# A four-layer graph network on one core: where the third chunk of layer 2 gets its first loads, and where pieces of layer 3 stand between its pairs

## The chip, the cores and the metric

The kernel runs on one core of one Trainium2 chip. TensorE (PE) multiplies matrices into PSUM, VectorE (DVE), ScalarE (ACT) and GpSimd (POOL) do the elementwise work, SyncE (SP) issues nearly all transfers from HBM. The metric is the device time of one execution in microseconds; the time of a kernel is the median of its runs.

## The reference

Four layers follow each other on 3327 nodes with 64 features; each adds its result to its input and normalises every row. All four use the same 3327 x 3327 matrix `adj`.

```python
# layer 0
neigh = jnp.matmul(adj, features) / (adj.sum(axis=1, keepdims=True) + 1.0)
x = _layernorm(x + jnp.concatenate([x, neigh], axis=-1) @ W.T)
# layer 1: w = adj / deg; agg = einsum('ij,ijc->ic', w, logmap(x_i, x_j)); then weight, bias, expmap
x = _layernorm(x + _L1_gnn_ref(x, adj, weight, bias))
# layer 2
deg = jnp.clip(jnp.sum(adj, axis=1, keepdims=True) + 1.0, 1.0, None)
h_neigh = (adj @ X + X) / deg
out = jax.nn.relu(jnp.concatenate([X, h_neigh], axis=1) @ W + b)
x = _layernorm(x + out / jnp.maximum(jnp.linalg.norm(out, axis=1, keepdims=True), 1e-12))
# layer 3
support = input @ weight
mask = (adj != 0)
rank = jnp.cumsum(mask, axis=1); deg = rank[:, -1:]; k = jnp.minimum(deg, 100.0)
pos = rank - (deg - k)
w = mask * jnp.where(pos > 0, 0.5 ** (k - pos), 0.0)
x = _layernorm(x + w @ support + bias)
```

## The kernel before

**Tiles and chunks.** The nodes are padded to 26 blocks of 128. `adj`, transposed by the host, is cut along its rows' nodes into four chunks of 832 columns. One load (`load_adj`, L289) brings a pair of blocks of one chunk, 128 x 2 x 832 numbers, 832 KB, into one of four buffers with the tag `adj`; a load into a list of two tiles (L285) is two transfers of one block each. All of these are on SP's queue, in the order in which the program makes them, and a load waits there until its buffer has been read.

**Layer 2** goes through the chunks in the order `ORDER2 = (2, 3, 1, 0)`: `n == 0` is chunk 2, `n == 1` chunk 3, `n == 2` chunk 1, `n == 3` chunk 0. In this document the first, second, third and fourth chunk are meant in that order. A chunk is 13 pairs; the place of a pair in its chunk's order is called its position, `i`. `aggregate_pair` (L455) multiplies one pair into an accumulator, with four matmuls, each of which stands in the trace as two rows. At the end of a chunk `keep_sums` copies the accumulator to SBUF (L439), and `epilogue2` multiplies the weights (L1226) and makes the features of that chunk's blocks, among them `parts`, a sum of three bfloat16 terms for layer 3.

**Ranks and masks.** Layer 3's weights come from ranks, which for the second chunk are counted while its pairs go by: DVE makes a mask of each pair (L481) in one of ten buffers with the tag `m16`, PE counts it (L527) two pairs later, DVE carries the count on (L513) and ACT writes the ranks (L537). The ranks' last row is mended by `last_rows`, with small DMAs on POOL's queue and three DVE steps (L554 to L556).

**Layer 3** is cut into 52 pieces, each a pair of blocks of one chunk. `expand` turns a piece's ranks into `bits` (L1288 on ACT, L1290 on DVE, also in `m16` buffers; the letters of `L3_ENGINES` and `L3_FIRST` name the engine), and `piece` multiplies them with `parts` in twelve matmuls (L1313). A piece needs the features of its two blocks alone, so pieces run beside layer 2: `L3_AMONG` says behind which positions of the third and fourth chunk one stands. The first piece makes nine pieces' bits before itself (`BITS_AHEAD`, `L3_FIRST`), which DVE and ACT begin behind the last mask and the last ranks; every piece then makes those of the ninth piece after it. Pieces 0 to 5 need blocks of the first chunk only, piece 6 is the first that needs a block of the second. The other pieces follow layer 2, and `epilogue3` ends each chunk: weights (L1330), sum with the features (L1337), squares (L403) into the one buffer `sq`, their sum (L404), a root (L417) with three short DVE steps (L418 to L420), the output (L1347) and its transfer (L1351). The last chunk is ended in two halves of three and four blocks.

The order of the work on an engine is the program's, rearranged when it is built by a planner with costs of its own; `issue_after` fixes the order of two instructions of one engine. At run time each engine keeps its order.

The edit touches `sum_of_squares` and `table_root` (which other epilogues also call, without the new arguments), and, inside `layers_2_and_3`, `epilogue2`, `expand`, `piece`, `epilogue3` and the loop over `ORDER2`.

Of the kernel before, what the change touches and what calls it, by code (L numbers as in the profile page):

```python
# [20 lines left out]
FP = mybir.dt.float32  # L21
# [4 lines left out]
AF = mybir.ActivationFunctionType  # L26
# [5 lines left out]
P = 128  # L32
NB = 26
NP = NB * P
D = 64
CH = 832
HC = CH // 2
NCH = NP // CH
# [6 lines left out]
GB = 7  # L45
# [53 lines left out]
L3_ENGINES = "VSVVS"  # L99
BITS_AHEAD = 9  # L100

L3_FIRST = "VVVVSVVSV"

L3_AMONG = {2: range(6, 13), 3: range(13)}


L3_LEFT = 16
# [5 lines left out]
def four_gnn_layers_kernel(  # L113
# [279 lines left out]
                issue_after(ins, behind)  # L393
        return True

    def sum_of_squares(y, nb, s, alone=False):

        width = y.shape[2]
        sq = small.tile([P, GB, D], FP, name="sq", tag="sq", bufs=1)
        if alone:  # L400
            nc.vector.tensor_mul(sq[:, 0:nb, 0:width], y, y)
        else:
            nc.scalar.activation(sq[:, 0:nb, 0:width], y, AF.Square)  # L403
        return nc.vector.tensor_reduce(s, sq[:, 0:nb, 0:width], axis=AX.X, op=ALU.add)  # L404

    def variance(s, work):
# [4 lines left out]

        return rsqrt(variance(s, work)[0], work)

    def table_root(s, work):

        y, h = work("root"), work("part")
        nc.scalar.activation(y, s, AF.Abs_reciprocal_sqrt, bias=ln_eps, scale=1.0 / D)  # L417
        nc.vector.scalar_tensor_tensor(h, s, D * LN_EPS, y, op0=ALU.add, op1=ALU.mult)  # L418
        nc.vector.tensor_mul(h, h, y)
        nc.vector.scalar_tensor_tensor(y, h, -3.0 * D, y, op0=ALU.add, op1=ALU.mult)  # L420
        return y
# [769 lines left out]
    def layers_2_and_3(banks, acc, done, rows, there):  # L1191


        with tc.tile_pool(name="l2m", bufs=10) as mp, tc.tile_pool(name="late", bufs=1) as late:
# [24 lines left out]
            def epilogue2(c, x2, behind=None):  # L1219


                b0, b1_, nb = blocks_of(c, GROUPS2)
                work, alone = Work(nb), c == ORDER2[-1]
                pb = per_block(banks.pair(2), nb, 2 * D)
                for k in range(nb):
                    issued = nc.tensor.matmul(  # L1226
                        pb[:, k, :], lhsT=sums[:, bass.ts(b0 + k, P)], rhs=wl2, start=True, stop=True
                    )
                    if behind is not None:
                        issue_after(issued, behind)  # L1230
# [12 lines left out]
                nc.vector.tensor_scalar_max(ss, ss, 1e-24)  # L1243
                r, k = (rsqrt(ss, work), 1.0) if alone else (table_norm(ss, work), 0.375)
                nc.vector.scalar_tensor_tensor(y, y, k, col(r, nb), op0=ALU.mult, op1=ALU.mult)
                aside.tensor_add(y, y, x2)
                ss = work("ss")
                sum_of_squares(y, nb, ss, alone)
                r, k = (deviation(ss, work), 1.0) if alone else (table_root(ss, work), -0.5 / D)
                left = node_tile("left")  # L1250
                copy = nc.vector.tensor_copy if alone else nc.scalar.copy

                for k0, k1 in ((0, 3), (3, nb)) if alone else ((0, nb),):
                    xs = x3[:, b0 + k0 : b0 + k1, :]
# [12 lines left out]
                aside.tensor_tensor(  # L1267
                    xs, xs, bias["b3"].to_broadcast([P, nb, D]), op=ALU.add
                )
                return issued  # L1270

            acc3, begun, bits_of, ranks_of = {}, set(), {}, {}

            def expand(k, behind=None):


                if k >= len(pieces):
                    return
                c, jp = pieces[k]
                bits = mp.tile([P, 2, CH], U16, name="bits", tag="m16")  # L1280
                src = last_rank if c == LATE_RANKS else rank[:, c]
                src = src[:, 2 * jp : 2 * jp + 2, :]
                bits_of[k] = bits
                engine = L3_FIRST[k] if k < len(L3_FIRST) else L3_ENGINES[k % len(L3_ENGINES)]
                if k in beside:
                    engine = "S"
                if engine == "S":
                    issued = nc.scalar.mul(bits, src, 128.0)  # L1288
                else:
                    issued = nc.vector.tensor_scalar(bits, src, 128.0, None, op0=ALU.mult)  # L1290
                if behind is not None:
                    issue_after(issued, behind[engine])
                    behind[engine] = issued

            def piece(k, behind=None):
                if not acc3:

                    for which in range(2):
                        two = banks.pair(which)
                        for half in range(2):  # L1300
                            acc3[ORDER2[which + 2 * half]] = two[:, half, :]
                    last = {"V": ranks_of[LATE_RANKS].carried, "S": ranks_of[LATE_RANKS].made}
                    for ahead in range(BITS_AHEAD):
                        expand(ahead, last)
                    step(late_rows, last["V"])
                    all_of(late_rows)
                expand(k + BITS_AHEAD)
                c, jp = pieces[k]
                bits, last = bits_of.pop(k), jp == LAST_PAIR
                for b in range(2):  # L1310
# [11 lines left out]
                begun.add(c)  # L1322
                return issued

            def epilogue3(b0, b1_, bank, behind):

                nb = b1_ - b0
                pt = per_block(bank, nb, D)
# [11 lines left out]
                )  # L1340
                work = Work(nb)
                ss = work("ss")
                sum_of_squares(y, nb, ss)
                r = table_root(ss, work)
                o = adjp.tile([P, 2, CH], FP, name="o", tag="adj").rearrange("p t c -> p (t c)")
                o = o[:, 0 : nb * D].rearrange("p (b f) -> p b f", f=D)
                nc.vector.scalar_tensor_tensor(  # L1347
                    o, y, -0.5 / D, col(r, nb), op0=ALU.mult, op1=ALU.mult
                )
# [19 lines left out]
            ahead = [half_of(wt, k) for k in range(2)] + [  # L1369
                [mp.tile([P, CH], FP, name="a1", tag="m16") for _ in range(2)] for _ in range(2)  # L1370
            ]
            ahead = [load_adj(ORDER2[1], NB // 2 - 1 - k, t) for k, t in enumerate(ahead)]
            k, made = 0, None
            for n, c in enumerate(ORDER2):
                if n > 0:
# [8 lines left out]
                for i, jp in enumerate(order):  # L1384
                    if n == 0 and i < EARLY:
                        continue
                    if n == 0 and jp in there:
                        a2 = there.pop(jp)
                    elif n == 1 and ahead:
                        a2 = ahead.pop(0)  # L1390
                    else:
                        a2 = load_adj(c, jp)
                    issued = aggregate_pair(acc, xr, a2, jp, i == 0, i == NB // 2 - 1, counted)
# [1 line left out]
                        made = epilogue2(ORDER2[0], x2, issued)  # L1395
                    if ranks:
                        mask = ranks.mask(jp, a2)
                        counted = count(masked, places, min(LATE_LAG, jp), issued)
                    if i == OWN2_AT:
                        x2, based = prologue2(c, issued)  # L1400
# [19 lines left out]
            for n in range(NCH + 1):  # L1420
                for i in range(4):
                    if n < NCH:
                        issued = piece(k)
                        k += 1
                    if n > 0 and i == (1 if n < NCH else 0):
                        b0, b1_, nb = blocks_of(ORDER2[n - 1], GROUPS2)
                        halves3 = ((b0, b0 + 3), (b0 + 3, b1_)) if n == NCH else ((b0, b1_),)
                        for half, blocks in enumerate(halves3):
                            epilogue3(
                                *blocks, banks.one((n + half) % 2), issued if n < NCH else None  # L1430
                            )
                if n < NCH:
                    keep_sums(ORDER2[n], acc3[ORDER2[n]], 0, True)

# [57 lines left out]
```

## Time and profile before

| | |
|---|---|
| median of three runs | 525.27 us (524.14 to 527.98) |
| profiled execution: time, span | 527.45 us, 525.7 us |
| busy in the span: PE, DVE, ACT, POOL | 92%, 74%, 63%, 34% |
| granted clock of PE, mean | 0.987 |
| moved by DMA | 132.52 MB, mean 252 GB/s |
| loads `adj` on SP | 137 of 832 KB, median 5.4 us from issue to landing |

The span runs from the first to the last instruction of the program; the time of the same execution is 1.75 us longer. Times inside the profile are us from the start of the span. A "busy" PE is one with a matmul in flight, and the modelled ends of matmuls overlap the starts of the next. A wait in the trace is put down to what came last.

In the span, layer 2's third chunk lies at about 403 to 440 us, the fourth at 442 to 477, the rest of layer 3 after it; the last output is issued at 522.1 us.

### The profile page before, as it was taken

How to read it: one execution, taken by the hardware profiler on the slowest of the kernel's cores; microseconds unless marked ns; L12 is line 12 of the kernel's file. 1: busy time of each engine (PE TensorE's matmuls, PEld its weight loads, DVE VectorE, ACT ScalarE, POOL GpSimd, SP SyncE). 2: the span in 40 equal slices, each digit the busy share in tenths (PEclk: the TensorE clock that was granted, in tenths of full speed). 3: DMA queues.
4: the chain of work that ended last, by engine and by line, in shares of the span. 5: the costliest groups of instructions: out<-in, count | busy, mean ns of one | idle time of the engine just before them, and what ended most of it. 6: DMA issues, size and time to landing. Idle time of an engine off the chain costs nothing.

```text
span 525.7 us, 8489 instructions
## 1 busy us (share of the span) xinstructions
PE 483.0 (92%) x3256; PEld 237.9 (45%) x3256; DVE 387.5 (74%) x705; ACT 333.7 (63%) x393; POOL 180.9 (34%) x150
## 2 busy tenths in 40 slices
PE   5999999998967999999999899899999889999993
PEld 3554344453432333433343344354564445556672
DVE  3565439879668978789789978978788956727744
ACT  1435545775868999878978896721387714337941
POOL 2001101112027788857877695600331112200000
PEclk9999999999988999999999999999999999999997
DMA  8999999998439677767866777499687898950002
GB/s 273 316 350 340 392 391 392 306 304 280 181 126 328 210 255 275 238 204 229 284 216 204 248 252 253 151 351 399 231 271 255 269 393 300 349 190 1 1 17 56
DMA packets 46179, 132.52 MB, mean 252 GB/s; under 512 B 6934, under 2 KB 7038, under 8 KB 46066
## 3 DMA queue, kind: packets, MB, share of 16 engines
q1 hardware_dynamic: 45602, 131.35, 72.2%
q0 software_dynamic: 384, 0.52, 0.3%
q8 instruction: 27, 0.44, 0.3%
q14 instruction: 22, 0.18, 0.1%
q10 hardware_dynamic: 144, 0.03, 0.0%
HBM read 130.86 MB, written 0.85 MB: 251 GB/s over the span
## 4 chain that ended last, share of the span: by engine, by line
PE 42%; DVE 16%; ACT 6%; issue 2%; DMA 1%; POOL 0%; ACTq 0%; DVEq 0%
PE two L1313 10%; PE one L455 9%; DVE p L834 7%; PE one L854 6%; PE two L823 6%; PE two L455 4%; DVE s L842 3%; ACT s L847 3%; ACT s L848 2%; PE two L527 2%; DMA adj<-in_adjt_dram 1%; PE two L1226 1%; PE one L1330 1%; PE two L891 1%; DVE mask L513 1%
## 5 line engine op out<-in xcount | busy, mean ns | idle before, releaser
L849 POOL TENSOR_TENSOR s<-s,p 128x832 f32<-128x832 f32 x67 | 130.1, 1957 | 45.4 <-ACT s L848 34.9
L834 DVE SCALAR_TENSOR_TENSOR p<-two,adj 128x832 f32<-128x832 f32 x100 | 101.0, 1018 | 18.3 <-issue 13.6
L823 PE MATMUL two<-uw 64*128 64x416 f32 x416 | 91.1, 552 | 13.6 <-DVE s L842 7.2
L537 ACT ACTIVATE rank<-two,last_bias 128x832 uint8<-128x832 f32 x78 | 71.7, 952 | 45.4 <-PE two L527 23.1
L455 PE MATMUL one<-adj,x0w 128*64 128x416 f32 x416 | 82.8, 524 | 2.8 <-DMA adj<-in_adjt_dram 1.4
L854 PE MATMUL one<-s,xu 128*64 128x416 f32 x416 | 85.2, 525 | 0.0
L847 ACT ACTIVATE s<-two,far_bias 128x832 f32<-128x832 f32 x67 | 63.6, 950 | 23.1 <-DVE p L834 20.7
L513 DVE SCALAR_TENSOR_TENSOR mask<-two,minus_last,mask 32x832 bf16<-32x832 f32 x48 | 52.5, 1093 | 30.1 <-PE two L527 25.9
L823 PEld LDWEIGHTS two<-uw 64*128 64x128 f32 x416 | 37.9, 191 | 67.0 <-PE one L854 22.6
L481 DVE TENSOR_SCALAR mask<-adj 128x1664 bf16<-128x1664 f32 x48 | 50.6, 1055 | 15.1 <-DMA adj<-in_adjt_dram 14.5
L527 PE MATMUL two<-mask,tri 128*64 128x416 bf16 x416 | 53.4, 346 | 8.7 <-DVE mask L513 6.3
L848 ACT ACTIVATE s<-s 128x832 f32<-128x832 f32 x67 | 60.1, 897 | 1.9
L455 PE MATMUL one<-adj,xr 128*64 128x416 f32 x280 | 57.6, 514 | 3.1 <-DMA adj<-in_adjt_dram 3.1
L1313 PE MATMUL two<-bits,parts 128*64 128x416 bf16 x624 | 59.0, 340 | 0.0
L854 PEld LDWEIGHTS one<-s,xu 128*64 128x64 f32 x416 | 25.8, 136 | 47.5 <-issue 46.0
L1313 PEld LDWEIGHTS <-parts 128*64 128x64 bf16 x624 | 35.1, 110 | 24.9 <-issue 8.3
L455 PEld LDWEIGHTS one<-adj,x0w 128*64 128x64 f32 x416 | 29.2, 138 | 35.3 <-issue 23.4
L527 PEld LDWEIGHTS <-tri 128*64 128x64 bf16 x416 | 25.8, 110 | 41.5 <-issue 23.1
L1288 ACT ACTIVATE bits<-rank 128x1664 uint16<-128x1664 uint8 x20 | 30.6, 1580 | 18.8 <-PE two L1313 18.8
L842 DVE SCALAR_TENSOR_TENSOR s<-two,p 128x832 f32<-128x832 f32 x37 | 37.6, 1016 | 3.0 <-ACT two L839 2.5
L839 ACT ACTIVATE two<-two,far_bias 128x832 f32<-128x832 f32 x37 | 34.0, 918 | 5.1 <-DVE p L834 4.9
L1290 DVE TENSOR_SCALAR bits<-rank 128x1664 uint16<-128x1664 uint8 x19 | 20.4, 1087 | 16.2 <-PE two L1313 16.0
(268 smaller groups left out, 471.0 us busy)
## 6 DMA issues: line engine op xcount, KB each, us to landing
adj<-in_adjt_dram SPq DMA_DIRECT2D x137, 832.0 KB, 5.4
uw<-in_adjt_dram SPq DMA_DIRECT2D x7, 832.0 KB, 7.2
sums<-in_adjt_dram SPq DMA_DIRECT2D x2, 832.0 KB, 5.9
p<-in_adjt_dram SPq DMA_DIRECT2D x4, 416.0 KB, 4.8
s<-in_adjt_dram SPq DMA_DIRECT2D x4, 416.0 KB, 7.0
a<-in_adjt_dram SPq DMA_DIRECT2D x4, 416.0 KB, 6.2
uw<-in_xt_dram SPq DMA_DIRECT2D x1, 640.0 KB, 10.7
out_dram<-o SPq DMA_DIRECT2D x3, 192.0 KB, 2.5
```

Of the source, the lines that this page charges most:

```text
L455: issued = nc.tensor.matmul(acc[h * D : (h + 1) * D, 0:HC], lhsT=x[:, 2 * jp + k, 0:D], rhs=a[:, bass.ts(h, HC)], start=(first and k == 1) ...
L513: ranks.carried = nc.vector.scalar_tensor_tensor(halves(last), ranks.after[P - 32 : P, :, 0:HC], minus_last[P - 32 : P, :], halves(last), ...
L527: issued = nc.tensor.matmul(counts[k][rows, h, 0:HC], lhsT=lhsT[:, rows], rhs=mask[:, of, bass.ts(h, HC)], start=lhsT is tri, stop=(k == 1 ...
L537: ranks.made = nc.scalar.activation(halves(ranks.rank[:, 2 * jp + k, :]), counts[k][:, :, 0:HC], AF.Relu, bias=last_bias,)
L823: issued = nc.tensor.matmul(v[:, h, 0:HC], lhsT=wt[rows, bass.ts(jb, P)], rhs=ut[rows, bass.ds(c * CH + h * HC, HC)], start=True, stop=True,)
L834: issued = nc.vector.scalar_tensor_tensor(halves(p), v, 0.25 - 0.5 * FD, halves(a), op0=ALU.add, op1=ALU.mult)
L842: return nc.vector.scalar_tensor_tensor(halves(s), v, FG, halves(p), op0=ALU.add, op1=ALU.mult)
L847: nc.scalar.activation(halves(s), v, AF.Square, bias=far_bias, scale=-2.0)
L848: nc.scalar.activation(s, s, AF.Copy, bias=FG)
L849: nc.gpsimd.tensor_mul(s, s, p)
L854: issued = nc.tensor.matmul(acc[h * D : (h + 1) * D, 0:HC], lhsT=xu[:, jb, 0:D], rhs=s[:, bass.ts(h, HC)], start=first, stop=last,)
L1313: issued = nc.tensor.matmul(acc3[c][h * D : (h + 1) * D, 0:HC], lhsT=parts[:, 2 * jp + b, bass.ts(part, D)], rhs=bits[:, b, bass.ts(h, HC) ...
```

## The change

- **Two pairs fetched ahead.** Behind the last mask of the second chunk, four single-block tiles are taken from the `m16` buffers and filled with positions 4 and 5 (`AHEAD3`) of the third chunk. These loads stand on SP's queue behind the second chunk's last load and ahead of the third chunk's first. The four `adj` buffers then serve the other eleven positions.
- **Pieces.** The seven pieces beside the third chunk stand behind positions 1, 3, 5, 7, 9, 11 and 12 instead of 6 to 12. Six pieces' bits instead of nine are made ahead; `L3_MADE` says how many are to be made by the time of each of the first seven pieces, and from the seventh on it is as before. DVE's bits of pieces 12 to 20 are put behind the second sum of squares of the second chunk's `epilogue2`.
- **The end.** In `epilogue3` the squares go into the unused half of the output's own tile instead of the one buffer `sq`, and the epilogue is a generator that stops behind the sum of the squares: both halves of the last chunk do their squares and sums first, then their roots and outputs, and each root is put behind the last square on ACT.

The order of the instructions moves with it in three more places: DVE does the three steps of `last_rows` between the first steps of the second chunk's `epilogue2` and the bits behind them; ACT has bits of more pieces ahead of that epilogue's second square and of its copy into `parts`; POOL sends the mended rank row before that epilogue's subtraction (L1242) and not behind it.

```diff
-L3_FIRST = "VVVVSVVSV"
-L3_AMONG = {2: range(6, 13), 3: range(13)}
+L3_FIRST = "VVSVSS"
+L3_MADE = (6, 6, 7, 8, 9, 11, 13)
+L3_LATER = 12
+AHEAD3 = (4, 5)
+L3_AMONG = {2: (1, 3, 5, 7, 9, 11, 12), 3: range(13)}
...
-    def sum_of_squares(y, nb, s, alone=False):
+    def sum_of_squares(y, nb, s, alone=False, sq=None, made=None):
         width = y.shape[2]
-        sq = small.tile([P, GB, D], FP, name="sq", tag="sq", bufs=1)
+        if sq is None:
+            sq = small.tile([P, GB, D], FP, name="sq", tag="sq", bufs=1)
         if alone:
             nc.vector.tensor_mul(sq[:, 0:nb, 0:width], y, y)
         else:
-            nc.scalar.activation(sq[:, 0:nb, 0:width], y, AF.Square)
+            squares = nc.scalar.activation(sq[:, 0:nb, 0:width], y, AF.Square)
+            if made is not None:
+                made.append(squares)
...
-    def table_root(s, work):
+    def table_root(s, work, behind=None):
...
+        if behind is not None:
+            issue_after(issued, behind)
...
-                sum_of_squares(y, nb, ss, alone)
+                summed.append(sum_of_squares(y, nb, ss, alone))
...
-            def expand(k, behind=None):
+            def expand(behind=None):
+                k = len(bits_made)
                 if k >= len(pieces):
-                    return
+                    return False
+                bits_made.append(k)
...
+                elif engine == "V" and L3_LATER <= k < L3_LATER + BITS_AHEAD:
+                    issue_after(issued, summed[1])
+                return True
...
-                    for ahead in range(BITS_AHEAD):
-                        expand(ahead, last)
+                    for _ in L3_FIRST:
+                        expand(last)
...
-                expand(k + BITS_AHEAD)
+                while len(bits_made) < (L3_MADE[k] if k < len(L3_MADE) else k + BITS_AHEAD + 1):
+                    if not expand():
+                        break
...
-                sum_of_squares(y, nb, ss)
-                r = table_root(ss, work)
                 o = adjp.tile([P, 2, CH], FP, name="o", tag="adj").rearrange("p t c -> p (t c)")
-                o = o[:, 0 : nb * D].rearrange("p (b f) -> p b f", f=D)
+                o = o[:, 0 : 2 * GB * D].rearrange("p (b f) -> p b f", f=D)
+                sum_of_squares(y, nb, ss, sq=o[:, GB : 2 * GB, :], made=made)
+                yield
+                r, o = table_root(ss, work, made[-1]), o[:, 0:nb, :]
...
-                    elif n == 1 and ahead:
-                        a2 = ahead.pop(0)
+                    elif (n, i) in ahead:
+                        a2 = ahead.pop((n, i))
...
                         mask = ranks.mask(jp, a2)
+                        for k3 in AHEAD3 if i == NB // 2 - 1 else ():
+                            t = [mp.tile([P, CH], FP, name="a1", tag="m16") for _ in range(2)]
+                            ahead[n + 1, k3] = load_adj(ORDER2[n + 1], PAIRS[k3], t)
...
+                        made, ends = [], []
                         for half, blocks in enumerate(halves3):
-                            epilogue3(
-                                *blocks, banks.one((n + half) % 2), issued if n < NCH else None
-                            )
+                            ends.append(epilogue3(
+                                *blocks, banks.one((n + half) % 2), issued if n < NCH else None, made
+                            ))
+                            next(ends[-1])
+                        for end in ends:
+                            all_of(end)
```

More of the change, by code (lines that the diff above doesn't have):

```diff
@@ L412, in deviation @@
         return rsqrt(variance(s, work)[0], work)
-    def table_root(s, work):
+    def table_root(s, work, behind=None):
         y, h = work("root"), work("part")
-        nc.scalar.activation(y, s, AF.Abs_reciprocal_sqrt, bias=ln_eps, scale=1.0 / D)
+        issued = nc.scalar.activation(y, s, AF.Abs_reciprocal_sqrt, bias=ln_eps, scale=1.0 / D)
+        if behind is not None:
+            issue_after(issued, behind)
         nc.vector.scalar_tensor_tensor(h, s, D * LN_EPS, y, op0=ALU.add, op1=ALU.mult)
@@ L1270, in epilogue2 @@
                 return issued
-            acc3, begun, bits_of, ranks_of = {}, set(), {}, {}
-            def expand(k, behind=None):
+            acc3, begun, bits_of, bits_made, ranks_of = {}, set(), {}, [], {}
+            summed = []
+            def expand(behind=None):
+                k = len(bits_made)
                 if k >= len(pieces):
-                    return
+                    return False
+                bits_made.append(k)
                 c, jp = pieces[k]
@@ L1323, in piece, with epilogue3 @@
                 return issued
-            def epilogue3(b0, b1_, bank, behind):
+            def epilogue3(b0, b1_, bank, behind, made):
                 nb = b1_ - b0
@@ L1371, in layers_2_and_3 @@
             ]
-            ahead = [load_adj(ORDER2[1], NB // 2 - 1 - k, t) for k, t in enumerate(ahead)]
+            ahead = {
+                (1, k): load_adj(ORDER2[1], NB // 2 - 1 - k, t) for k, t in enumerate(ahead)
+            }
             k, made = 0, None
```

## The prediction

> **What bounds the kernel now.** I read first the engines' busy time by stretches of the span, to find where TensorE (PE) stops; then the chain of work that ended last, to see what it stops for; then PE's timeline for the size of the stops; then the landing times of single loads. The columns below are the stretch in us, its length, the busy us of PE, PE's weight loads, VectorE (DVE), ScalarE (ACT) and GpSimd (POOL), the granted clock, the DMA share and GB/s.
>
> ```profile
> 410.00:415.00 5.00, 5.00 (x38) 3.05 (x35) 4.97 (x7) 4.98 (x5) 0.51 (x1) 1.00 0.82 279
> 415.00:420.00 5.00, 3.53 (x20) 1.29 (x18) 5.00 (x11) 2.34 (x4) 0.61 (x1) 1.00 0.94 306
> 420.00:425.00 5.00, 3.38 (x26) 1.47 (x24) 2.52 (x7) 0.00 (x0) 2.66 (x3) 1.00 1.03 409
> 425.00:430.00 5.00, 5.00 (x44) 2.62 (x42) 1.12 (x2) 2.06 (x2) 0.00 (x0) 1.00 1.03 374
> ```
>
> From 425 on PE is full, and it stays full until 513.5 us. Only 415 to 425 has holes in this stretch, while the DMA engines are full. The chain (start, length, what) says whom PE waits for:
>
> ```profile
> 412.44 2.25 PE one L455 x11
> ...
> 414.71 7.42 DMA adj<-in_adjt_dram
> ...
> 422.18 1.62 PE one L455 x8
> 423.79 1.05 PE two L1313 x12
> 424.85 1.40 PE one L455 x8
> ```
>
> This is the third chunk (`n == 2` in the loop over `ORDER2`). A pair of matrix blocks costs PE 1.40 us, a piece of layer 3 1.05 us. Positions 0 to 6 of the chunk run as pairs alone, faster than loads arrive; all seven pieces come behind positions 6 to 12. PE's timeline has both stops, and, earlier, position 0 of the chunk, which the order puts at 403.24, between the last counts of the second chunk:
>
> ```profile
> 403.24 1.56 PE L455 MATMUL one<-adj,xr 128*64 128x416 f32 x6
> 404.88 0.54 PE L527 MATMUL two<-mask,tri 128*64 128x416 bf16 x4
> ...
> 412.37 5.10 PE L455 MATMUL one<-adj,xr 128*64 128x416 f32 x26
> 418.94 1.62 PE L455 MATMUL one<-adj,xr 128*64 128x416 f32 x8 [1.47 <-DMA adj<-in_adjt_dram]
> 422.18 1.62 PE L455 MATMUL one<-adj,xr 128*64 128x416 f32 x8 [1.61 <-DMA adj<-in_adjt_dram]
> ```
>
> The brackets give 3.08 us of idling, but modelled ends overlap the next start, so I count starts. A pair is 8 rows in 1.40 us, so the 26 rows from 412.37 take 4.55 and the pair of 418.94 could have started at 416.92: 2.02 lost. The next could have started at 420.34 instead of 422.18: 1.84 lost. **Together 3.86 us**, on a PE that is full for 88 us afterwards: what is saved here reaches the end.
>
> **The change part by part.**
>
> *Pieces behind positions 1, 3, 5, 7, 9, 11, 12, and positions 4 and 5 fetched ahead.* The number of pairs, pieces and bytes stays. PE from 412.37 is then: rest of position 1 (0.35), piece, positions 2 and 3 (2.80), piece, 4 and 5 (2.80), piece, so that position 6 is wanted at 412.37 + 0.35 + 3 x 1.05 + 5.60 = 421.47 and position 7 at 422.87. The four `adj` buffers now go to positions 0 to 3 and then 6, 7, 8, 9. The load issued at 409.3, position 4's before, is position 6's after and should land near 414; the one of 413.3, which landed after 5.6 us, is position 7's. Positions 8 and 9 get their buffers when 2 and 3 end (415.2 and 416.6) and are wanted at 425.3 and 426.7: ten us each, against a longest landing of 8.9. Position 10 follows position 6: issued 422.9, wanted at 429.2, 6.3 us; 11 and 12 have 7.1. A load takes 4.4 to 4.7 us from issue when the queue is short. So both stops go: -3.86.
>
> *What the early loads push back.* SP issues the four single-block loads of `AHEAD3` right behind the second chunk's last load (392.5) and ahead of position 0's (395.0). The issues cost nothing: four in the same form started 0.45 us apart, 392.9 + 1.8 = 394.7, and position 0's load waits for PE until 395.0 anyway. The transfers do cost: position 0 is behind 1.70 MB more.
>
> ```profile
> L289 SPq DMA_DIRECT2D adj<-in_adjt_dram x1: 368/368/368, 390.0 to 390.0; - x1
> DMA to landing us min/median/max: 4.6/4.6/4.6
> ...
> L289 SPq DMA_DIRECT2D adj<-in_adjt_dram x1: 367/367/367, 395.0 to 395.0; - x1
> DMA to landing us min/median/max: 5.4/5.4/5.4
> ...
> L289 SPq DMA_DIRECT2D adj<-in_adjt_dram x1: 367/367/367, 397.4 to 397.4; - x1
> DMA to landing us min/median/max: 6.0/6.0/6.0
> ```
>
> The load before the last of the second chunk lands at 394.65. Behind it are the last one, two pairs ahead, and position 0: four pairs. With a filled queue the loads issued at 417.5, 420.6 and 423.8 landed (8.9, 8.3 and 7.2 us later) at 426.4, 428.9 and 431.0: 2.3 us a pair. That gives 394.65 + 4 x 2.3 = 403.85 for position 0, wanted at 403.24: PE stops **+0.6 us**, and as PE has only 0.1 us of slack up to the last counts, all behind it moves. Lower bound: 2.08 us a pair (0.852 MB at the 409 GB/s of 420 to 425) gives 402.97, no stop. Upper bound: the loads of 395.0 and 397.4 landed 3.0 us apart, giving 406.65, a stop of 3.4. The filled queue is the nearest row, as the queue will be filled. Positions 1 and 2 move back by as much and are wanted at 408.4 and 413.8, five and more us later.
>
> A rule speaks against this step: the Trainium skill, "DMA: Bandwidth & Descriptors", section "Bandwidth" (Measured), gives 341 GB/s for 1 MB and advises at least 1 MiB a transfer, and the early loads are split into 0.43 MB. By 341 GB/s, an estimate from that page, the two pairs take 5.0 us instead of the 4.6 above, and the stop would be 1.0. This trace has four single-block loads back to back; two, issued at 361.3 and 361.8, landed after 6.2 and 6.8 us, 1.1 us apart, so 4.4 for four: the row does not show the penalty.
>
> *Masks' places for bits.* `L3_FIRST` makes six instead of nine pieces' bits ahead, since four of ten `m16` buffers hold the early pairs. Priced at nothing: piece 0 needs bits that DVE makes at 409.39 to 410.4, and the last ACT read of the PSUM bank it writes, 412.17; PE reaches it at 412.72. That cover is only 0.55 us; beyond it each us late costs a us, as the pairs queue behind the piece. Bits 6 need position 4's buffer (419.0) and are used at 435; by piece 7 as many are ahead as before.
>
> *Order on DVE, ACT and POOL.* DVE drops bits between the steps of the second chunk's `epilogue2`, but now puts `last_rows` there, which waits for a small POOL DMA that landed near 415.7; ACT puts bits that wait for PE before its root and before its copy into `parts`. Followed step by step with the durations of before, the last `parts` of that chunk come near 433.6 instead of 437.9, and piece 6, the first to need them, is wanted at 435.2. Priced at nothing, with 1.6 us of cover. POOL sends the corrected rank row ahead of its subtraction, some 4 us sooner; nobody waits for it yet.
>
> *The end: squares apart.* Only the last group matters; the others run under pieces.
>
> ```profile
> 518.42 0.36 ACT L403 ACTIVATE sq<-y 128x192 f32<-128x192 f32 x1 [0.83 <-DVE y L1337]
> 519.58 0.30 ACT L417 ACTIVATE root<-ss,ln_eps 128x3 f32<-128x3 f32 x1 [0.80 <-DVE ss L404]
> 519.79 0.40 ACT L403 ACTIVATE sq<-y 128x256 f32<-128x256 f32 x1
> 520.67 0.30 ACT L417 ACTIVATE root<-ss,ln_eps 128x4 f32<-128x4 f32 x1 [0.48 <-DVE ss L404]
> ```
>
> The second square (519.79) had its input at 519.29, but waited for the one `sq` buffer, read until 519.55. After, it runs 519.3 to 519.7, its sum to 520.2, the second root to 520.5. But the first half's three short DVE steps now stand behind that sum, 0.2 us each, then part 0.1, output 0.36, two more steps: the last output starts at 521.4 instead of 521.60: **-0.2**. Bounds: 0 (DVE's order eats it) and -0.5 (the square's own advance).
>
> **Sum.** -3.86 + 0.6 - 0.2 = -3.5 us. The profiled execution has a span of 525.7 and a time of 527.45; it would become 522.2 and 523.95. The profiled execution lies at the slow end of the three timed runs (524.14 to 527.98, median 525.27); the forecast on the median is 525.27 - 3.5 = **521.8 us**. Its own range, with the bounds of the two unknown terms and half a us of the runs' scatter, is 520 to 525.
>
> **The rivals.**
>
> *The early loads cost most of what they save.* With the 3.0 us a pair of 395 to 403, position 0 stops PE for 3.4 us: -3.86 + 3.4 - 0.2 = -0.7, 524.6. For it: those two landings. Against it: in that stretch the queue held one or two loads, so each began on idle engines; a filled queue later ran at 2.3.
>
> *The wait moves instead of going.* Position 10 has 6.3 us from issue to use, and landings of 7.2 to 8.9 exist. At 7.8 it is 1.5 late: -3.5 + 1.5 = -2.0, 523.3. For it: the same four buffers, refilled at PE's pace. Against it: the long landings stood behind two or three others; after the change 8 and 9 have landed when 10 is issued.
>
> *Slower.* The same place as the first rival, with a rate below any pair of landings shown here: position 0 blocks PE, the counts behind it, and with them the bits. From a landing at 407.3 on, 3.2 us a pair, the stop exceeds the 4.06 saved. At 3.5 us a pair it lands at 408.65, a stop of 5.4: -3.86 + 5.4 - 0.2 = +1.3, 526.6. Against it: 3.5 us a pair is 243 GB/s, which the DMA engines run at only with gaps, and a filled queue has none.
>
> **How the numbers follow.** Forecast 0.66, first rival 0.14, moved wait 0.13, slower 0.07. A change of about 1%, 5.3 us, is what a measurement of this kernel can tell from none. Faster by that needs 520.0 or less: the bounds at their best give 3.86 + 0.5 = 4.4, 520.9, so only with the runs' scatter: 0.14. Slower by that needs 530.5: part of the last rival, 0.05. The rest, 0.81, is within. The range goes from the best bound less a us of scatter, 519.7, to the first rival and some scatter, 525.4.
>
> **What would show it.** Right: no DMA wait on PE between 412 and 436; the line of pieces between pairs from about 413; a stop of under 1 us before position 0; the second chunk's last `parts` before piece 6; the second square at the end ahead of the first root. Wrong: a stop of 2 us or more near 403, a DMA wait at position 10 or later, or PE waiting for DVE or ACT before piece 0 or 6.

## The result, and the profile after

The kernel after takes 523.72 us (median of 14 runs, 521.61 to 526.32), against 528.6 us of the kernel before, timed beside it (14 runs, 524.14 to 532.57). The ratio is 0.992, with a 95% interval of 0.9895 to 0.9948: 0.8% faster, about 4 us, and "within 1%". The range of the forecast holds the time, the forecast itself is 1.9 us below it. The forecast stood on the median of three runs of the kernel before, 525.27; these three are the first of the fourteen, and two of them are the fastest of these. So the ratio says more than the distance to 521.8: taken off 528.6, the forecast gain of 3.5 us gives 525.1.

The profiled execution has a span of 521.7 us where that of before had 525.7. Read in the same order as before, the busy time by stretches has no hole of PE left (the columns are the stretch, its length, the busy us of PE, PE's weight loads, DVE, ACT and POOL, the granted clock, the DMA share, GB/s):

```profile
405.00:410.00 5.00, 5.00 (x42) 2.59 (x44) 3.35 (x4) 4.66 (x6) 0.00 (x0) 1.00 0.87 297
410.00:415.00 5.00, 5.00 (x45) 3.57 (x42) 4.39 (x7) 4.99 (x5) 0.51 (x1) 1.00 0.86 284
415.00:420.00 5.00, 5.00 (x38) 2.99 (x36) 4.93 (x10) 4.07 (x6) 1.45 (x2) 1.00 0.96 333
420.00:425.00 5.00, 5.00 (x41) 3.02 (x37) 3.55 (x10) 3.29 (x3) 1.13 (x1) 1.00 0.66 179
425.00:430.00 5.00, 5.00 (x42) 3.21 (x38) 2.98 (x7) 0.51 (x2) 0.00 (x0) 1.00 0.87 306
```

Two columns tell the story. PE's 3.53 and 3.38 of 415 to 425 have become 5.00. And the DMA engines, full in 420 to 425 before (409 GB/s), have slack there now (179), because more was moved ahead of it. The first two rows are of before, the third is of after:

```profile
400.00:405.00 5.00, 4.83 (x34) 2.24 (x34) 4.73 (x7) 3.44 (x5) 1.70 (x2) 1.00 0.73 252
405.00:410.00 5.00, 5.00 (x44) 2.57 (x44) 3.38 (x4) 4.66 (x6) 0.00 (x0) 1.00 0.40 116
400.00:405.00 5.00, 4.82 (x34) 2.21 (x34) 4.76 (x7) 3.43 (x5) 1.71 (x2) 1.00 1.03 408
```

In 400 to 410 the kernel after moves 3.5 MB (408 and 297 GB/s) where the kernel before moved 1.8 (252 and 116): the difference, 1.7 MB, is as much as the two early pairs hold. The chain of work that ended last (start, length, what) has no DMA between the weights of the second chunk (L1238) and those of the third:

```profile
410.70 1.76 PE two L1238 x14
412.46 0.30 PE one L467
412.76 0.35 PE two L1333 x2
...
414.19 2.50 PE one L467 x14
416.68 0.18 PE two L1333
...
431.15 0.78 PE two L1216 x6
431.93 1.55 PE one L467 x8
433.47 1.06 PE two L1333 x12
434.53 1.40 PE one L467 x8
435.93 1.05 PE two L1333 x12
436.98 1.53 PE two L1238 x12
```

The chain first has a matmul of piece 0 at 412.76 (on PE's timeline the first starts at 412.40, beside the last of position 1), and the pieces stand between pairs from there on. At the end both halves' squares now lie ahead of both roots (ACT's timeline):

```profile
514.54 0.36 ACT L411 ACTIVATE o<-y 128x192 f32<-128x192 f32 x1 [0.77 <-DVE y L1358]
515.55 0.42 ACT L411 ACTIVATE o<-y 128x256 f32<-128x256 f32 x1 [0.65 <-DVE y L1358]
515.87 0.28 ACT L427 ACTIVATE root<-ss,ln_eps 128x3 f32<-128x3 f32 x1
516.45 0.30 ACT L427 ACTIVATE root<-ss,ln_eps 128x4 f32<-128x4 f32 x1 [0.30 <-DVE ss L414]
```

To see where the 4 us come from, I take in each profile the times at which PE starts the weights of each chunk of layer 2 and of each group of layer 3, and compare the steps between them. Whole spans can't be compared as closely: the first of these marks lies anywhere between 373.4 and 379.8 us in the executions of this study.

| from weights to weights, us | before | after | difference |
|---|---|---|---|
| first to second chunk | 35.08 | 35.10 | 0 |
| **second to third chunk** | 29.77 | 26.27 | **-3.50** |
| third to fourth, fourth to layer 3's first group | 34.57, 25.09 | 34.56, 25.09 | 0 |
| layer 3's groups 1 to 2, 2 to 3 | 5.86, 6.04 | 5.86, 6.04 | 0 |
| **layer 3's groups 3 to 4** | 5.12 | 4.77 | **-0.35** |
| **last weights to the last output's start on DVE** | 4.54 | 4.34 | **-0.20** |

The three differences sum to 4.05 us; the spans differ by 4.0.

### The profile page after: what moved, and what is told of

It reads as the page before. It is cut to its first block, busy times and chain, and to the rows that moved or that the text cites. A ratio compares the mean times of both kernels' runs of the same rounds, so it can differ in the third digit from the quotient of the medians.

```text
span 521.7 us, 8496 instructions
## 1 busy us (share of the span) xinstructions
PE 482.3 (92%) x3256; PEld 240.5 (46%) x3256; DVE 387.0 (74%) x703; ACT 336.7 (65%) x395; POOL 180.1 (35%) x150
## 4 chain that ended last, share of the span: by engine, by line
PE 53%; DVE 24%; ACT 10%; DMA 6%; issue 3%; POOL 0%; ACTq 0%; DVEq 0%
PE one L467 16%; PE two L1333 10%; DVE p L846 8%; PE two L835 7%; DMA adj<-in_adjt_dram 6%; PE one L866 6%; PE two L539 5%; DVE mask L525 4%; PE two L467 4%; ACT s L859 3%; DVE s L854 3%; DVE mask L493 3%; ACT s L860 2%; ACT rank L549 2%; PE two L1238 1%
## 5 line engine op out<-in xcount | busy, mean ns | idle before, releaser
L1333 PE MATMUL two<-bits,parts 128*64 128x416 bf16 x624 | 62.3, 339 | 0.0
L1333 PEld LDWEIGHTS <-parts 128*64 128x64 bf16 x624 | 36.8, 110 | 24.2 <-issue 7.3
L1303 ACT ACTIVATE bits<-rank 128x1664 uint16<-128x1664 uint8 x22 | 33.6, 1579 | 15.5 <-PE two L1333 14.6
L549 ACT ACTIVATE uw<-two,last_bias 128x832 uint8<-128x832 f32 x26 | 24.2, 950 | 12.5 <-DVE mask L525 6.4
```

Source lines behind the costliest of these rows:

```text
L549: ranks.made = nc.scalar.activation(halves(ranks.rank[:, 2 * jp + k, :]), counts[k][:, :, 0:HC], AF.Relu, bias=last_bias,)
L1333: issued = nc.tensor.matmul(acc3[c][h * D : (h + 1) * D, 0:HC], lhsT=parts[:, 2 * jp + b, bass.ts(part, D)], rhs=bits[:, b, bass.ts(h, HC) ...
```

## The experiments

The experiments vary the three parts: the fetch ahead, the places of the pieces, the end. "The third chunk's stretch" is the step from the second chunk's weights to the third's.

**Pieces alone.** The two pairs aren't fetched ahead.

```diff
-AHEAD3 = (4, 5)
+AHEAD3 = ()
```

> The changed kernel without the two pairs fetched ahead; the pieces stay behind positions 1, 3, 5, 7, 9, 11 and 12, six pieces' bits are made ahead, the end is as changed. Theory A (supply: the stage stops because pairs are wanted faster than four buffers are refilled, and either more pairs in place or pieces in between cure it): positions 4 and 5 are wanted near 417.6 and 419.0 and their loads land near 414 and 418 to 419; position 6 is wanted at 421.5, issued at 415 to 416 and landing near 421; position 7 lands near 424 and is wanted at 423: a stop of 0.3 to 1.5 us remains, and the stage between the second and the third chunk's weights takes 26.6 to 28 us (29.8 before, 26.3 changed). Span 522.0 to 523.4. Theory B (only the two extra pairs matter): both stops stay, stage 29 us or more, span 524.5 or more. Theory C (only the pieces' places matter): as the changed kernel, stage 26.3, span 521.7.

Measured: stretch 27.36, ratio to the kernel before 0.9955 (0.9933 to 0.998). PE still waits for DMA twice. The first view is the waits of PE between 400 and 445 us (us in total, times, longest), the rest PE's timeline:

```profile
PE one L467 <- DMA adj<-in_adjt_dram: 0.6, 2, 0.5
```

```profile
427.33 1.62 PE L467 MATMUL one<-adj,xr 128*64 128x416 f32 x8 [0.49 <-DMA adj<-in_adjt_dram]
...
431.55 1.62 PE L467 MATMUL one<-adj,xr 128*64 128x416 f32 x8 [0.15 <-DMA adj<-in_adjt_dram]
```

So spreading the pieces removes most of the stop, not all of it: the stretch is 1.1 longer than in the kernel after.

**Fetch alone.** The pieces stand behind positions 6 to 12, as before the change.

```diff
-L3_AMONG = {2: (1, 3, 5, 7, 9, 11, 12), 3: range(13)}
+L3_AMONG = {2: range(6, 13), 3: range(13)}
```

> The changed kernel with the pieces beside the third chunk back behind positions 6 to 12; two pairs are fetched ahead, six pieces' bits are made ahead, the end is as changed. Theory A: positions 2 to 5 go through without a piece, position 6 is wanted at 418.3 and its load lands near 414.3; 7 is wanted at 420.8 (lands 418), 8 at 423.2 (421), 9 at 425.7 (424): no stop of PE, stage of 25.9 to 26.3 us, span 521.3 to 521.7. Theory C (only the pieces' places matter): pairs alone outrun the loads again at position 6 or 7, a stop of 1.5 us or more, span 523 or more.

Measured: stretch 26.24, no DMA wait, ratio 0.9916 (0.989 to 0.994). The fetch does by itself what both do together.

**Neither**: both edits above at once, so that the six bits, the new order on DVE, ACT and POOL, and the end are left.

> The kernel after without the two early pairs and with the pieces at their old places: what is left is six pieces' bits made ahead instead of nine, the new order on DVE, ACT and POOL, and the end. Theory A (the new order is free where masks' places are not wanted by loads): the third chunk's stretch is that of the kernel before, 28.7 to 30.0 us, with two DMA waits of PE behind position 4 and 5, and the third to the fourth group takes 4.77; the time is 0 to 0.5 us below the kernel before, ratio 0.998 to 1.000. Theory B (the order itself brings part of the 3.5 us, because ACT and DVE free buffers earlier): the stretch is below 28.5, ratio about 0.996.

Measured: stretch 29.37, third to fourth group 4.77, and PE waits for DMA as before:

```profile
PE one L467 <- DMA adj<-in_adjt_dram: 2.3, 2, 2.1
```

The ratio, 0.9965 (0.9935 to 0.9996), is a little below what A gave, though its interval reaches into it; the stages say A, since the stretch is that of before. The stretch shows no gain from the order of the small work by itself.

**One pair ahead**, position 4 alone, with the pieces at their old places; run twice.

```diff
-AHEAD3 = (4, 5)
+AHEAD3 = (4,)
-L3_AMONG = {2: (1, 3, 5, 7, 9, 11, 12), 3: range(13)}
+L3_AMONG = {2: range(6, 13), 3: range(13)}
```

> As the kernel with the pieces behind positions 6 to 12 and two pairs fetched ahead, but with one pair, position 4, fetched ahead. Theory A (supply): position 5 now has the load of 409.3 (lands near 414), 6 that of 413.3 (lands 418 to 419, wanted at 418.3), 7 one issued at 415.8 (lands near 421.5, wanted at 420.8), 8 one issued at 417.2 (lands near 424, wanted at 423.2): stops of 0.7 to 1.7 us in all, the third chunk's stretch 27.0 to 28.0 us against 26.24 with two pairs and 29.8 with none. A theory by which what counts is something else that came with the early loads (six pieces' bits, the order on DVE and ACT) expects 26.2.

Measured: stretch 26.34 and no wait of PE for DMA, which misses the expectation; but the ratio, 0.998 (0.995 to 1.001), showed nothing of this gain, and the profiled execution, 521.84 us, was the fastest of the twelve timed (median 526.14). Its timeline of weight loads shows how near the stop was: those of position 6 waited for its load, and the stretch is still only 0.1 longer than with two pairs ahead.

```profile
416.63 0.20 PEld L467 LDWEIGHTS one<-adj,xr 128*64 128x64 f32 x4 [0.60 <-DMA adj<-in_adjt_dram]
```

Another execution of the same kernel:

> The kernel with one early pair (position 4) and the pieces at their old places, once more, for another profiled execution. Theory A (position 7's load lands within some tenths of a us of its use, so that single executions stop and others don't): a wait of PE for DMA of 0 to 1 us before position 7, and a third chunk's stretch of 26.3 to 27.3. Theory B (one early pair is enough, always): 26.2 to 26.4 again, no DMA wait between 412 and 436.

Measured: stretch 27.85, 0.55 more than the expectation allowed, with these rows on PE's timeline:

```profile
417.28 1.90 PE L467 MATMUL one<-adj,xr 128*64 128x416 f32 x7
420.55 1.62 PE L467 MATMUL one<-adj,xr 128*64 128x416 f32 x8 [1.36 <-DMA adj<-in_adjt_dram]
422.00 1.23 PE L1333 MATMUL two<-bits,parts 128*64 128x416 bf16 x12
```

The stop comes ahead of position 6, not of position 7 as the expectation had it: the pair of 420.55 is the one that the first piece (L1333) follows. Its load, issued at 413.63, landed after 6.9 us, near 420.5. One pair puts position 6's load at the edge: one execution stops for it, another doesn't. The first profile alone would have told the wrong story; the timed runs warned of it.

**The end alone.** The kernel before with the squares apart, nothing else.

```diff
...
-                sum_of_squares(y, nb, ss)
-                r = table_root(ss, work)
...
+                sum_of_squares(y, nb, ss, sq=o[:, GB : 2 * GB, :], made=made)
+                yield
+                r, o = table_root(ss, work, made[-1]), o[:, 0:nb, :]
...
```

> The kernel before with the changed end alone: squares into the output's tile, both halves' squares before their roots. By the prediction's step only the last group gains, 0.2 us: span 525.5. If the wait of 0.34 us before the third group's square, which is gone in the changed kernel, also comes from the one buffer for squares, the gain is 0.55: span 525.15. If that wait came from elsewhere, it is still there in this run.

Measured: third to fourth group 4.77, last weights to last output 4.34, ratio 0.999 (0.997 to 1.001); the stretch 30.02.

**All but the end**: the kernel after with the old `epilogue3`.

> The changed kernel with the end of before: one buffer for squares, each half of the last group by itself. By the prediction's step 0.2 us slower than the changed kernel: span 521.9. If the wait of 0.34 us before the third group's square comes back with the one buffer: span 522.25, and the difference between the weights of the third and the fourth group is 5.12 us instead of 4.77.

Measured: stretch 26.27, last weights to last output 4.54, ratio 0.9925 (0.990 to 0.995). The end's 0.2 is there with the edit and gone without it. But third to fourth group takes 4.82, not 5.12: most of that 0.35 does not belong to the new tile.

**The kernel before once more.**

> The kernel before once more. If the wait of 0.34 us before the third group's square in its first profile belongs to the kernel, the weights of the third and the fourth group are 5.12 us apart again; if it was a chance of that execution, 4.82 as in the changed kernel with the old end. The third chunk's stretch should be 29.8 to 30.0 again.

Measured: stretch 28.72, third to fourth group 5.11. So the 5.12 repeats, and the stretch doesn't: over the five executions with the old order of loads and pieces and the old bits (both of the kernel before, the end alone, and the last two below) it is 29.77, 28.72, 30.02, 28.94 and 29.12.

**The early loads where the prediction had them.** In the kernel after they are not where the prediction put them; SP's row for them reads

```profile
L291 SPq DMA_DIRECT2D a<-in_adjt_dram x4: 424/448/1202, 397.8 to 400.1; - x4
...
DMA to landing us min/median/max: 6.0/6.8/7.2
```

that is behind the loads of positions 0 and 1 (395.0 and 397.4), not ahead of them. This experiment puts them ahead.

```diff
...
-        nc.sync.dma_start(out=t, in_=adjt[c, 2 * jp : 2 * jp + 2].rearrange("b p i -> p b i"))
+        issued = nc.sync.dma_start(out=t, in_=adjt[c, 2 * jp : 2 * jp + 2].rearrange("b p i -> p b i"))
+        if behind is not None:
+            issue_after(issued, behind)
...
-                        a2 = load_adj(c, jp)
+                        a2 = load_adj(c, jp, None, early[-1] if n == 2 and i < 2 else None)
```

> The changed kernel with one order added on SP's queue: the loads of the third chunk's positions 0 and 1 behind the four early single-block loads, the place where the prediction put these (in the changed kernel they stand behind position 1's load). By the prediction's step position 0 then lands 0.6 us after PE wants it (bounds 0 and 3.4): the stretch from the first to the second chunk's weights, 35.1 us in both kernels, becomes 35.7 (35.1 to 38.5), the next stays 26.3, span up by 0.6. If a filled queue moves a pair in 2.08 us there is no stop and the place costs nothing. If the early loads also have to wait on SP for their masks to be counted, position 0's load is issued later than 395 and the stop is 1 to 3.5 us.

Measured: position 0's load lands at 404.93; the step to the second chunk takes 34.96 and the stretch 28.35, together 1.94 more than in the kernel after; ratio 0.997 (0.994 to 1.001). The planner takes position 0 out of the hole between the counts, and PE idles there instead (its timeline):

```profile
402.97 0.54 PE L543 MATMUL two<-mask,tri 128*64 128x416 bf16 x4
404.96 0.54 PE L543 MATMUL two<-mask,tri 128*64 128x416 bf16 x4 [1.45 <-DVE mask L529]
```

So half of the whole gain hangs on a place in SP's queue that the diff does not write down. The 1.94 include the planner's answer to that place. Had position 0 kept its own, PE would have waited for it from 403.26 to 404.93, about 1.7 (an estimate from these times; no run has that order).

**The copy first**, for a better version: fetch alone, and in the groups before the last the copy of the sums stands ahead of the root's short steps on DVE.

```diff
...
-        nc.vector.scalar_tensor_tensor(h, s, D * LN_EPS, y, op0=ALU.add, op1=ALU.mult)
+        issued = nc.vector.scalar_tensor_tensor(h, s, D * LN_EPS, y, op0=ALU.add, op1=ALU.mult)
+        if copied is not None:
+            issue_after(issued, copied)
...
```

> Pieces behind positions 6 to 12, two pairs fetched ahead, the changed end, and in the groups before the last the sums' copy ahead of the root's short steps on DVE (their root and output come after the copy). In the changed kernel PE ends the last piece's matmuls near 512.2 and the copy starts at 512.60, behind three short steps that wait for ACT's root. With the copy first it starts near 512.3: the weights of the third and the fourth group 4.45 us apart instead of 4.77, the rest as in the kernel with the pairs fetched ahead and the old places; 0.3 us less than that kernel. Rival: the postponed root and output (1.1 us on DVE) push the last group's first sum, and nothing is gained.

Measured: stretch 26.24, third to fourth group 4.46, 0.31 less than in the kernel after; ratio 0.993 (0.9895 to 0.996). The copy (L453) now comes before the three steps (L430 to L434; DVE's timeline):

```profile
514.85 0.58 DVE L453 COPY sums<-two 64x416 f32<-64x416 f32 x1 [0.54 <-PE two L1335]
515.36 0.15 DVE L430 SCALAR_TENSOR_TENSOR part<-ss,root 128x6 f32<-128x6 f32 x1
```

By its stages this is the fastest version of all; by its timed runs it can't be told from the kernel after.

**The 0.35 between the third and the fourth group.** In the kernel before, the third group's square starts late. This row of ACT's timeline is that of before; in the kernel after and in all but the end the bracket reads 2.76:

```profile
514.47 0.52 ACT L403 ACTIVATE sq<-y 128x384 f32<-128x384 f32 x1 [3.05 <-DVE y L1337]
```

The semaphore instruction that it follows was released at 514.12 and took 0.02, so 0.34 pass in which it waits for nothing that the profile shows ("issue" in the chain of before); elsewhere this step takes 0.05.

```profile
514.12 0.02 ACTq L403
514.13 0.34 issue
514.47 0.53 ACT sq L403
```

Two variations of the kernel before shift ACT's count of instructions (the second gives DVE one more).

```diff
+    spare = const.tile([P, 1], FP, name="spare")
+    for _ in range(2):
+        nc.scalar.copy(spare, far_bias)
```

> The kernel before, and ACT copies a constant into an unused tile of one column twice at the start of the program, 400 us and more ahead of the place in question. In the kernel before, the third group's square on ACT starts 0.34 us after the semaphore instruction that it follows was released, and a packet of instructions arrives 0.63 us behind its start; elsewhere such a start takes 0.05. Theory A (at this instruction ACT crosses into its next block of instructions, so that any shift of ACT's count moves the delay to another instruction): with two more instructions ahead, the crossing falls two instructions earlier, where ACT waits for PE anyway; the square starts 0.05 us after its release, and the third to the fourth group takes 4.8 us instead of 5.12. Theory B (the delay belongs to this instruction or to its buffer): 0.34 and 5.1 again.

Measured: the delay is gone, third to fourth group 4.82.

```profile
515.74 0.52 ACT L406 ACTIVATE sq<-y 128x384 f32<-128x384 f32 x1 [2.76 <-DVE y L1340]
```

```diff
-            nc.scalar.copy(wl1[D : 2 * D, 0:D], tp[0:D, 0, 0:D])
+            nc.vector.tensor_copy(wl1[D : 2 * D, 0:D], tp[0:D, 0, 0:D])
```

> The kernel before, with one copy of 64 x 64 numbers in the preparation of layer 2's weights on DVE instead of ACT, so that ACT has one instruction less ahead of the place in question. Theory A (ACT's crossing into its next block): the delay moves one instruction later, from the third group's square to its root; the square starts 0.05 us after its release, the root 0.9 to 1.0 us after the square's end instead of 0.62, and the third to the fourth group stays at 5.1 us. Theory B (the delay belongs to the square or to its buffer): the square late by 0.34 as before, the root at 0.62.

Measured: the delay is gone here too, 4.82, and the root follows after 0.62 as ever:

```profile
513.93 0.52 ACT L403 ACTIVATE sq<-y 128x384 f32<-128x384 f32 x1 [2.76 <-DVE y L1337]
515.08 0.30 ACT L417 ACTIVATE root<-ss,ln_eps 128x6 f32<-128x6 f32 x1 [0.62 <-DVE ss L404]
```

Theory B is out: the square and its buffer are the same, and the delay goes with one instruction less as with two more. Of theory A the square came as forecast, the root and the stage (5.1 forecast) did not: nothing of the delay shows at the root. The root waits for DVE until 515.08 anyway, so a delay of 0.34 behind the square's start at 513.93 would be over in time; this cover is worked out, not measured.

## Why the prediction was right, and where it was not

**The two stops, -3.86: right in kind, 0.36 too much.** The stage measured -3.50. The mis-sized step is "the 26 rows from 412.37 take 4.55". The row itself says otherwise: it is 5.10 long, and its last matmul 0.51 of that, so that its starts spread over 4.59, and 26 rows two by two need only 12 x 0.35 = 4.2 between the first and the last start. A pair's matmuls run side by side on two column halves of the array (their starts are 0.01 us apart), but the two rows that are left of position 1 stand on one half alone. PE's timeline of the kernel after shows it, since there a piece (L1333) starts beside them:

```profile
412.39 0.56 PE L467 MATMUL one<-adj,xr 128*64 128x416 f32 x1
412.40 0.71 PE L1333 MATMUL two<-bits,parts 128*64 128x416 bf16 x3
412.79 0.51 PE L467 MATMUL one<-adj,xr 128*64 128x416 f32 x1
```

So in the kernel before 14 of the 26 rows are on one half and 12 on the other. The last one starts at 416.96, and the pair of 418.94 could have started at 417.31 at the earliest, not 416.92. The first stop was 1.63. With 1.84 for the second that gives 3.47. (A third load was late too, position 4's: at 415.54 the half that is ahead waits 0.3 us for it, which costs nothing.) The kernel after pays the same 0.35 elsewhere: position 10, which the transposes (L1216) follow, shows 1.57 us for seven rows (429.58 in the chain), where at 1.40 for eight they would take 1.22. The brackets, 3.08, erred by more, in the other direction.

The 3.5 belong to the profiled execution of before. Over the five executions with the old order the stretch averages 29.31, 3.05 above the 26.26 of the four executions with both early pairs in the planner's places (the kernel after, fetch alone, all but the end, the copy first).

**What the early loads push back, +0.6: did not occur.** The step that failed is "SP issues the four single-block loads right behind the second chunk's last load (392.5) and ahead of position 0's (395.0)"; the description of the change ahead of the prediction has the same sentence, and it is wrong. Their places in the program are those, but the planner put them behind position 1's load. Position 0 therefore runs where it ran, at 403.26 (before: 403.24). I took the order of SP's queue from the order in the source. At the assumed place they cost 1.94, inside the bounds of 0 to 3.4 but three times the value taken: the estimate saw the late landing (404.93 against a forecast of 403.85) but not that PE's order would change and that the masks and counts behind it would wait.

**The rule on small transfers.** The four early loads, 0.426 MB each, landed at 403.86, 404.93, 405.99 and 407.05: 1.06 us apart, 401 GB/s. The 4.6 us assumed for two pairs were 4.25. Where they were put first they landed 1.27 us apart, with other loads among them: the engines moved 413 GB/s in 395 to 400 and 396 in 400 to 405. The Trainium skill's "DMA: Bandwidth & Descriptors", section "Bandwidth", gives 341 GB/s for a transfer of 1 MB and asks for at least 1 MiB a transfer; loads of 0.426 MB that follow each other on a filled queue did not show that penalty, and the measurement decides.

**The waits that did not come.** The loads of positions 6 and 7 were issued at 409.3 and 413.3 and landed after 5.0 and 4.8 us, at 414.3 and 418.1 (forecast: near 414, and after 5.6 us). Position 10's, the one that the second rival feared, was issued at 423.49 and landed after 4.5, near 428.0; its pair begins at 428.94, so this rival was 0.9 us away. PE waits for no engine and no transfer between 412 and 436.

**The steps priced at nothing held.** Piece 0 starts at 412.40 (forecast 412.72) without a wait for bits. The last `parts` end at 434.1 (forecast 433.6), piece 6 starts at 435.75 (435.2). "Neither" shows no gain and no loss from the order alone.

**The end, -0.2: right**, in size (4.54 to 4.34, the same within 0.01 in every kernel that has it against every one that hasn't) and in its steps: counted from the fourth group's weights, the last output comes 0.2 sooner behind the order on DVE that was forecast.

**What was missed: -0.35 between the third and the fourth group.** "Only the last group matters; the others run under pieces" is the failed step: fourteen matmuls of the fourth group's weights wait for the copy of their sums, which on DVE stands behind the third group's root. The new tile gives 0.05 of it (4.82 to 4.77): the semaphore instruction ahead of the square no longer waits for DVE, but is through 3.2 us sooner. 0.30 is the delay on ACT, which was lost because the change gave ACT another number of instructions ahead of that place.

In sum the profile gave -3.50 + 0 - 0.20 - 0.35 where the prediction had -3.86 + 0.6 - 0.2; a gain put 0.36 too high stands against a price of 0.6 that wasn't paid and a gain of 0.35 that wasn't seen, and 0.6 us are left between the two sums. That they lie so near is in part luck, and so is the nearness of 521.8: it stands on a base 3.3 us below the median of the fourteen runs, and this error and the gain put too low go opposite ways. Of the rivals, none came true: the early loads cost nothing, no wait moved, and nothing was slower. One thing that the prediction did not ask was whether both edits were needed. They weren't: the fetch alone gives all that the stretch gained.

## What to carry to other kernels

Where loads are late once in a stretch, count the bytes that can be moved in the quieter stretch ahead of it before rearranging the work that waits; here two pairs early did all of it, and seven moved pieces alone left 1.1 us. When a scheduler orders the issues, read the queue's real order: the same four loads cost nothing behind two others and 1.9 us ahead of them, the planner's rearrangement included. And measure a stop in several executions, since one profile of an edge case may show none.

## What the hardware showed unexpectedly

- **A delay that belongs to an instruction's number.** ACT's 0.34 us were there in both executions of the kernel before and vanished when two instructions were added or one taken away hundreds of us ahead. A packet of instructions arrives at 515.10, 0.98 behind the release of 514.12, which suggests that ACT went on to a new block of instructions there. The packet moves with the count: with one instruction less it arrives at 514.92, 0.99 behind the square's start, with two more at 510.99, 1.00 behind the start of the second group's square. That delay and packet go by ACT's count is shown; that fetching is the mechanism is argued. The Trainium skill, "Runtime: NRT & Kernel Launch", section "Instruction fetch mechanics", says that crossing a block of 256 instructions is mostly hidden; here, if it was that, it was not.
- **One half of the array stays behind the other.** Two matmul rows of position 1, left on one half, cost 0.35 us once, and not where they stand: before at the next stop, after at the transposes, some 18 us later.
- **The same stop varies by 1.3 us** between executions of the same order of loads (28.72 to 30.02), while each of the table's other steps up to the third group repeats within 0.03 in all fourteen profiles, leaving aside the one where position 0 was moved.
